# Gated cross-attention and mixture feed-forward: x^T from DRAM, normalized in place, instead of transposes of normalized x

## The chip, the core and the metric

The kernel runs on one core of one Trainium2 chip. A core has a matrix engine (TensorE: PE for its matmuls, PEld for its weight loads), a vector engine (VectorE, DVE), a scalar engine (ScalarE, ACT), a general engine (GpSimd, POOL) and SyncE (SP), which here issues almost all DMAs. Each engine runs its own list of instructions in order and waits for the others through semaphores. The DMAs are carried out by 16 DMA engines. The metric is the device time of one execution in microseconds (us); less is better.

## What is computed

For each of 8 batches, with x of 256 tokens by 512 features and a context of the same shape:

```
x = x + tanh(g0) * attention(layernorm(x), context)
x = x + tanh(g1) * ffn(layernorm(x))

attention(h, c): q = concat(c, h) @ Wq            (32 heads of 16)
                 k, v = h @ Wk, h @ Wv ; ck, cv = c @ Wsk, c @ Wsv   (8 heads of 16)
                 causal window of 64 tokens over both sets of keys, linear bias, softmax
                 output @ Wo
ffn(h):          8 gated (SiLU) basis pieces mixed by a top-4 router, plus a shared gated part
layernorm(x) = (x - mean) / sqrt(var + 1e-5), over the 512 features, without weights
```

Everything is float32. Only the first layernorm, the one ahead of the attention's projections, is touched by the change.

## The kernel before

The host part of the kernel lays some inputs out anew, without arithmetic: the context is handed over already transposed (features by tokens). All matmuls that project x contract over features, so they need normalized x with features on the 128 partitions; this is the tile xnT, 4 blocks of 128 features by 256 tokens, 4 KB in each partition.

**Order of the work.** The kernel writes its instruction order out by hand. Generators (Python functions that yield a cost) emit the instructions of one stage each, and `run` always advances the generator whose time is least. Time is counted in batches: 1.0 is one batch of feed-forward. `start(gen, length, at, total)` stretches a generator so that `total` yielded units take `length` of a batch. Three kinds of generator overlap: `feed_forward(b)` fills the batch's time from b to b + 1; `attention(b + 1)` starts at b - 0.2 and takes 0.86; `project(b + 2)` starts at b + 0.01 (batch 2's at -0.06) and takes 0.62 for 60 units. So in the steady state TensorE alternates between feed-forward blocks of batch b, attention of batch b + 1 and projections of batch b + 2.

**The projections (`project`).** For b of 2 and more: wait until batch b - 3 is stored, load x (L112, 512 KB) and the transposed context ctT (L118, 512 KB) on SP, yield 16 units; then `norm` (L179 to L184): two bn_stats and bn_aggr on DVE, an addition of epsilon on DVE, and a power of -0.5 on POOL; 3 units later `normed` (L190) writes normalized x, two 128x512 tensor_scalar on DVE; 3 units later, for each half of 128 tokens, `transposed` issues four TensorE transposes into one PSUM bank (L204, tile tr_x) and a copy on ACT brings them to xnT (L205). Then come the keys (L532, context first, then xnT), four groups of queries (L584), and the values (L604). All of them share one PSUM bank, `ps_one`, which `hold` and `give` hand from user to user; the tail of the attention (L888 and on) uses it too. Batch 0 is projected by `project_first` and batch 1 by `project` with rows normalized earlier; these keep the transposes.

**Buffers that matter here.** xnT comes from a pool with two buffers (tag "xo") in which it alternates with oT, the attention's output; x has three buffers, ctT one.

**The feed-forward.** Ten pieces a batch, each a set of blocks on TensorE (L1023, L1032) with weight halves that SP loads from DRAM (`load_gu`, L349 and L351). Each weight buffer exists twice: `after` issues the load for piece i + 2 as soon as piece i's last block with that buffer has been emitted. DVE, ACT and POOL follow with sums (L1068, L1079, L1091 on DVE; L1069, L1070 on POOL), tanh (L985 on ACT), gates (L990 on DVE), products (L1108 on DVE) and an accumulation (L1113 on POOL). In batch 0, sums of weights are also made (L975 on DVE and POOL) and kept in DRAM (L979 on SP) for the later batches.

**The attention.** Scores on TensorE (L650) into four PSUM banks; DVE adds the bias and takes the maximum (L663); ACT takes exponentials (L682); DVE's reciprocal (L691) and POOL's multiplication (L694) normalize; DVE transposes 32x32 blocks (L707); TensorE multiplies with the values (L729), which SP has spread into a block-diagonal tile in sixteen DMAs a batch (L496).

Of the kernel before, what the change touches and what calls it, by code (L numbers as in the profile page):

```python
# [9 lines left out]
F32 = mybir.dt.float32  # L10
# [5 lines left out]
P = 128  # L16
# [21 lines left out]
def gated_block(  # L38
    ctx: ExitStack,
    tc: tile.TileContext,  # L40
    x: bass.AP,
    context_t: bass.AP,
    g_xattn: bass.AP,
    g_ffn: bass.AP,
# [65 lines left out]
    def load(b, eng=nc.sync):  # L110
        xt = three.tile([P, NT, HID], F32, tag="x", name=f"x_{b}")
        eng.dma_start(xt, x[b].rearrange("(t p) d -> p t d", p=P))  # L112
        return xt
# [219 lines left out]
    }  # L333

    summed = set()

    def load_gu(i, g):

# [162 lines left out]
    def put_values(pv):  # L501
# [2 lines left out]
            pv.rearrange("p t s (k d) -> p (t s) k d", d=D),  # L504
        )

    def project(b, xns=None):
        def own():
            yield from hold(0.0 if b == 1 else GAP)

        def bank(shape, name):
            return ps_one.tile(shape, F32, tag="one", name=name)

        free = give
        if b > 1:
            while b > 2 and b - 3 not in stored:
                yield 0.5
            loaded[b] = load(b), load_context(b)
            yield 16.0
        xt, ctT = loaded[b]  # L520
        if xns is None:
            normed = norm(xt, range(NT), f"a{b}")
            yield 3.0
            xns = normed()
            yield 3.0
        xnT = two.tile([P, NC, T], F32, tag="xo", name=f"xnT_{b}")
        kT = two.tile([P, 2, 2, T], F32, tag="kT", name=f"kT_{b}")

        def keys(pk, s):
            w_sb, src = ((wsk_sb, ctT), (wk_sb, xnT))[s]  # L530
            for c in range(NC):
                nc.tensor.matmul(  # L532
                    pk[:, s, :], lhsT=w_sb[:, c, :], rhs=src[:, c, :],
                    start=(c == 0), stop=(c == NC - 1),
                )

        if b == 1:

            yield BEFORE
            yield from own()  # L540
            pk = bank([P, 2, T], f"pk_{b}")
            keys(pk, 0)
            for t in range(NT):
                yield MORE
                evict = transposed(
                    xnT, xns[t], t, f"x{b}",
                    lambda shape, name: other_bank(2, name).rearrange("p (c n) -> p c n", n=P),
                )
                yield AFTER
                evict()  # L550
            yield BEFORE
            keys(pk, 1)
            yield AFTER
        else:
            for t in range(NT):
                yield from own()
                evict = transposed(xnT, xns[t], t, f"x{b}", bank)
                yield AFTER - 0.8
                evict()
                free()  # L560
                yield BEFORE + 0.8
            yield from own()
            pk = bank([P, 2, T], f"pk_{b}")
            for s in range(2):
                keys(pk, s)
                yield AFTER

        for par in range(2):
            for s in range(2):
                nc.scalar.activation(  # L570
                    kT[:, par, s, :], pk[:, s, :], AF.Copy, scale=kmask[:, par : par + 1],
                )
        free()
        yield BEFORE
        if b == 1:
            yield BEFORE


        qT = two.tile([P, NB, G, Q], F32, tag="qT", name=f"qT_{b}")
        for g in range(G):  # L580
            yield from own()
            pq = bank([P, T], f"pq_{b}_{g}")
            for c in range(2 * NC):
                nc.tensor.matmul(  # L584
                    pq, lhsT=wq_sb[:, c, g * P : (g + 1) * P],
                    rhs=(ctT if c < NC else xnT)[:, c % NC, :],
                    start=(c == 0), stop=(c == 2 * NC - 1),
                )
                if c % NC == NC - 1:
                    yield MORE if c < NC else AFTER  # L590
            nc.scalar.activation(
                qT[:, :, g, :], pq.rearrange("p (b q) -> p b q", q=Q), AF.Copy, scale=-0.25
            )
            free()
            yield BEFORE
        projected[b] = kT, qT


        yield from own()
        pv = bank([P, NT, 2, HK * D], f"pv_{b}")  # L600
        for t in range(NT):
            for s, (w_sb, src) in enumerate(((wsv_sb, ctT), (wv_sb, xnT))):
                for c in range(NC):
                    nc.tensor.matmul(  # L604
                        pv[:, t, s, :], lhsT=src[:, c, t * P : (t + 1) * P], rhs=w_sb[:, c, :],
                        start=(c == 0), stop=(c == NC - 1),
                    )
            yield AFTER if t else MORE
        put_values(pv)
        free()  # L610
        yield BEFORE
# [668 lines left out]


_INS = [
    "x", "ctx_2048", "g_xattn", "g_ffn",
    "L0_xattn_Wq", "L0_xattn_Wk", "L0_xattn_Wv", "L0_xattn_Wsk", "L0_xattn_Wsv", "L0_xattn_Wo",
    "L0_ffn_w_router", "L0_ffn_w_gate", "L0_ffn_w_up", "L0_ffn_w_down",
    "L0_ffn_amplitudes", "L0_ffn_expert_scale",
# [32 lines left out]
```

## Time and profile before

| | us |
|---|---|
| median of 3 runs | 1020.11 |
| lowest and highest of them | 1019.47 and 1020.87 |
| span of the profiled execution, first to last instruction | 1016.5 |
| what lies around it (median less span) | 3.6 |
| DVE, ACT, POOL busy in that span | 597.9, 441.4, 469.3 |
| TensorE transposes of x (tr_x): 64 matmuls of 128x128, busy in all | 10.1 |
| moved by DMA in that span | 192.15 MB, 189 GB/s |

The profiled execution's own device time is not listed apart from the runs, so its span stands for it. TensorE's granted clock has a mean of 0.988 of full speed. How to read the rows that follow: a group of instructions has its line in the kernel, engine, operation, tiles written and read (out<-in, buffer numbers left out), shapes and count; a row of the timeline has its start and length in us, and in square brackets how long the engine idled just before and what ended that. A row of stretches has its bounds, its length, the busy time of PE, PEld, DVE, ACT and POOL, the granted clock, the DMA engines' busy share and GB/s. The chain of work that ended last is followed back from the last instruction, at each step to what released it.

### The profile page before, as it was taken

How to read it: one execution, taken by the hardware profiler on the slowest of the kernel's cores; microseconds unless marked ns; L12 is line 12 of the kernel's file. 1: busy time of each engine (PE TensorE's matmuls, PEld its weight loads, DVE VectorE, ACT ScalarE, POOL GpSimd, SP SyncE). 2: the span in 40 equal slices, each digit the busy share in tenths (PEclk: the TensorE clock that was granted, in tenths of full speed). 3: DMA queues.
4: the chain of work that ended last, by engine and by line, in shares of the span. 5: the costliest groups of instructions: out<-in, count | busy, mean ns of one | idle time of the engine just before them, and what ended most of it. 6: DMA issues, size and time to landing. Idle time of an engine off the chain costs nothing.

```text
span 1016.5 us, 27831 instructions
## 1 busy us (share of the span) xinstructions
PE 989.0 (97%) x10470; PEld 801.1 (79%) x10470; DVE 597.9 (59%) x2241; ACT 441.4 (43%) x1657; POOL 469.3 (46%) x892
## 2 busy tenths in 40 slices
PE   8899799999999999999999999999999999999998
PEld 8768587867888787886878868787787967787885
DVE  2765666657563775536755377545766466765453
ACT  3653354336542464425643255433654245542231
POOL 4773485635543265423634236432455234661341
PEclk9899799999999999999999999999999999999999
DMA  6943854578444794547844586455864468665891
GB/s 208 239 148 105 222 162 145 178 220 276 155 140 146 201 310 123 166 143 214 270 146 147 167 228 229 137 156 175 268 201 136 146 189 251 205 191 174 275 303 64
DMA packets 117302, 192.15 MB, mean 189 GB/s; under 512 B 12848, under 2 KB 34864, under 8 KB 117168
## 3 DMA queue, kind: packets, MB, share of 16 engines
q1 hardware_dynamic: 112672, 184.87, 58.3%
q10 hardware_dynamic: 4112, 4.46, 1.3%
q8 instruction: 83, 1.36, 0.5%
q0 software_dynamic: 384, 1.05, 0.5%
q14 instruction: 51, 0.42, 0.1%
HBM read 158.87 MB, written 14.68 MB: 171 GB/s over the span
## 4 chain that ended last, share of the span: by engine, by line
PE 88%; DVE 6%; DMA 2%; ACT 2%; POOL 1%; issue 1%; SPq 0%; ACTq 0%; DVEq 0%; POOLq 0%
PE m L1023 37%; PE pq L584 9%; PE m L1032 9%; PE sc L729 6%; PE po L888 5%; PE sc L650 5%; PE pd L1166 4%; PE pv L604 3%; PE pk L532 2%; PE pd L1169 2%; PE pq L402 1%; PE pl L918 1%; DMA ctT<-in_ctx 1%; DVE pr L663 1%; PE tr_f L204 1%; PE tr_x L204 1%
## 5 line engine op out<-in xcount | busy, mean ns | idle before, releaser
L694 POOL TENSOR_SCALAR pr<-pr,rd 128x192 f32<-128x192 f32 (+2 forms) x512 | 209.6, 428 | 228.9 <-DVE rd L691 202.5
L682 ACT ACTIVATE pr<-pr,nm 128x192 f32<-128x192 f32 (+2 forms) x512 | 218.9, 430 | 96.5 <-DVE nm L663 54.0
L1023 PE MATMUL m<-w,sT 128*128 128x256 f32 x1024 | 253.0, 381 | 7.0 <-DMA w<-in_L_ffn_w_up 7.0
L1023 PEld LDWEIGHTS m<-w,sT 128*128 128x128 f32 x1024 | 194.5, 191 | 34.2 <-DMA w<-in_L_ffn_w_up 7.4
L663 DVE CUSTOM_DVE_ANT_1 pr<-sc,nbias 128x192 f32<-128x192 f32 (+2 forms) x512 | 153.9, 322 | 90.3 <-PE sc L650 83.3
L1023 PE MATMUL m<-w,hT 128*128 128x256 f32 x768 | 203.9, 388 | 1.1 <-DVE u L1068 1.0
L1023 PEld LDWEIGHTS m<-w,hT 128*128 128x128 f32 x768 | 139.5, 190 | 25.8 <-issue 6.6
L1113 POOL TENSOR_TENSOR mixed<-mixed,th 128x256 f32<-128x256 f32 x112 | 82.2, 734 | 149.2 <-DVE th L1108 149.2
L707 DVE STREAM_TRANSPOSE pt<-pr 128x768 f32<-128x768 f32 (+2 forms) x128 | 111.5, 871 | 4.0 <-POOL pr L694 3.3
L682 ACT ACTIVATION_READ_ACCUMULATOR pr<-pr,nm 128x1 f32 x512 | 98.0, 191 | 0.0
L985 ACT ACTIVATE th<-m 128x256 f32<-128x256 f32 x80 | 30.8, 386 | 150.9 <-DVE up L1079 150.9
L1069 POOL TENSOR_TENSOR m<-m,u 128x256 f32<-128x256 f32 x80 | 60.6, 757 | 63.9 <-DVE u L1068 54.9
L1091 DVE TENSOR_TENSOR gate<-u,m 128x256 f32<-128x256 f32 x80 | 33.3, 416 | 81.2 <-PE m L1023 71.5
L729 PEld LDWEIGHTS sc<-pt,vbd 64*32 64x32 f32 x5120 | 62.5, 109 | 20.5 <-issue 11.2
L650 PE MATMUL sc<-kT,qT 32*128 32x192 f32 (+2 forms) x1024 | 67.2, 342 | 6.5 <-DVE nm L663 6.1
L729 PE MATMUL sc<-pt,vbd 64*32 64x96 f32 (+2 forms) x5120 | 70.2, 235 | 3.0 <-DVE pt L707 2.1
L1079 DVE TENSOR_TENSOR up<-u,m 128x256 f32<-128x256 f32 x80 | 33.2, 414 | 66.5 <-PE m L1023 40.0
L650 PEld LDWEIGHTS sc<-kT,qT 32*128 32x128 f32 x1024 | 46.7, 187 | 29.1 <-DVE nm L663 9.7
L985 ACT ACTIVATE th<-gate 128x256 f32<-128x256 f32 x80 | 33.3, 417 | 81.7 <-DVE gate L1091 81.6
L1032 PE MATMUL m<-sT,w 128*128 128x128 f32 x512 | 65.1, 275 | 0.0
L1032 PEld LDWEIGHTS m<-sT,w 128*128 128x128 f32 x512 | 61.6, 192 | 0.4
L1070 POOL TENSOR_TENSOR m<-m,m 128x256 f32<-128x256 f32 x80 | 58.5, 731 | 6.3
(131 smaller groups left out, 1373.6 us busy)
## 6 DMA issues: line engine op xcount, KB each, us to landing
w<-s SPq DMA_DIRECT2D x284, 256.0 KB, 3.3
w<-in_L_ffn_w_gate SPq DMA_DIRECT2D x130, 256.0 KB, 3.0
w<-in_L_ffn_w_up SPq DMA_DIRECT2D x73, 256.0 KB, 4.0
vbd<-vpad SPq DMA_DIRECT2D x120, 128.0 KB, 3.0
s<-w SPq DMA_DIRECT2D x40, 256.0 KB, 3.3
w<-in_L_ffn_shared_w_gate SPq DMA_DIRECT2D x32, 256.0 KB, 2.7
w<-in_L_ffn_shared_w_up SPq DMA_DIRECT2D x18, 256.0 KB, 3.5
sd<-in_L_ffn_shared_w_down SPq DMA_DIRECT2D x16, 256.0 KB, 3.6
```

What stands on the lines that cost most here:

```text
L584: nc.tensor.matmul(pq, lhsT=wq_sb[:, c, g * P : (g + 1) * P], rhs=(ctT if c < NC else xnT)[:, c % NC, :], start=(c == 0), stop=(c == 2 * N ...
L650: nc.tensor.matmul(seen(scs[p][:, j * COLS : (j + 1) * COLS], qb), lhsT=qT[rows, qb].rearrange("p g q -> p (g q)"), rhs=kT[rows, par, :, f ...
L663: nc.vector.tensor_tensor_reduce(out=part, in0=seen(scs[p][:, j * COLS : (j + 1) * COLS], qb0 + j), in1=bass.AP(tensor=bias.tensor, offset ...
L682: nc.scalar.activation(part, part, AF.Exp, bias=nmax, scale=-1.0, accum_out=den)
L694: nc.gpsimd.tensor_scalar(part, part, rden[:, p : p + 1], 1.0, op0=ALU.mult, op1=ALU.mult)
L707: nc.vector.transpose(pt[:, u % 4].rearrange("p c (s k) -> p (c s) k", s=2)[:, :, lo:], pr.rearrange("p c (s k) -> p (c s) k", s=2)[:, :, ...
L729: nc.tensor.matmul(scs[gp][32 * c : 32 * (c + 1), 2 * COLS + lo * Q : 2 * COLS + hi * Q], lhsT=vbd[rows, kb % (P // Q), kb // (P // Q) * 2 ...
L985: nc.scalar.activation(th, gate, AF.Tanh, scale=0.5)
L1023: nc.tensor.matmul(dst, lhsT=sides_of[m][c], rhs=w[:, c, :], start=(first and c == 0), stop=(c == NC // 2 - 1), skip_group_check=True,)
L1032: nc.tensor.matmul(dst[:, cols], lhsT=w[:, c, cols], rhs=sides_of[m][c], start=(first and ic == c == 0), stop=(c == NC // 2 - 1), skip_gro ...
L1069: nc.gpsimd.tensor_add(m7, m7, u)
L1113: nc.gpsimd.tensor_add(mixed[t], mixed[t], th)
```

## The change

For batches 2 to 7, x is handed over a second time, transposed by the host (`x_t`), and SP loads it straight into xnT, right behind x and ctT. Row statistics are taken as before from x (tokens on partitions). Mean and reciprocal deviation, 4 values in each partition, are stored to DRAM in an order in which they form one row of 512 values for each batch, and that row is loaded back into all 128 partitions (tile wide, 256 KB). DVE then subtracts the means from xnT in place and POOL multiplies by the deviations, each in two halves of 128x512. The transposes, their copies and the two normalizing instructions are gone for these batches. Seven units lie between the store and the first subtraction, 2.1 behind each half. To make room for wide, the area in SBUF for descriptors of POOL's DMAs is cut to 8192 bytes a partition. Batches 0 and 1 are as before.

```diff
+    rows = {b: sums.tile([NT, 2, P], F32, tag=f"rows{b}", name=f"rows{b}") for b in range(2, B)}
...
+    def norm_transposed(b, xt, xnT):
+
+        stats = small.tile([P, NT, 6], F32, tag="stats", name=f"st_a{b}")
+        mr = small.tile([P, NT, 2], F32, tag="mv", name=f"mv_a{b}")
+        for t in range(NT):
+            nc.vector.bn_stats(stats[:, t, :], xt[:, t, :])
+            nc.vector.bn_aggr(mr[:, t, :], stats[:, t, :])
+        veps = small.tile([P, NT], F32, tag="veps", name=f"ve_a{b}")
+        nc.vector.tensor_scalar(veps, mr[:, :, 1], LN_EPS, None, op0=ALU.add)
+        nc.gpsimd.tensor_tensor(mr[:, :, 1], veps, neghalf, ALU.pow)
+        nc.sync.dma_start(rows[b].rearrange("t s p -> p (t s)"), mr.rearrange("p t s -> p (t s)"))
+        wide = one.tile([P, NT, 2, P], F32, tag="wide", name=f"wide_{b}")
+        nc.sync.dma_start(
+            wide.rearrange("p t s n -> p (t s n)"),
+            rows[b].rearrange("t s p -> (t s p)").partition_broadcast(P),
+        )
+        yield 7.0
+        for half in range(2):
+            part = xnT[:, half * NC // 2 : (half + 1) * NC // 2, :].rearrange(
+                "p c (t n) -> p c t n", t=NT
+            )
+            for which, eng, op in ((0, nc.vector, ALU.subtract), (1, nc.gpsimd, ALU.mult)):
+                row = wide[:, :, which, :]
+                eng.tensor_tensor(
+                    part, part,
+                    bass.AP(
+                        tensor=row.tensor, offset=row.offset,
+                        ap=[list(row.ap[0]), [0, NC // 2], [2 * P, NT], [1, P]],
+                    ),
+                    op,
+                )
+            yield 2.1
...
             loaded[b] = load(b), load_context(b)
+            xnT = two.tile([P, NC, T], F32, tag="xo", name=f"xnT_{b}")
+            nc.sync.dma_start(xnT, x_t[b].rearrange("(c p) t -> p c t", p=P))
             yield 16.0
-        xt, ctT = loaded[b]
-        if xns is None:
-            normed = norm(xt, range(NT), f"a{b}")
-            yield 3.0
-            xns = normed()
-            yield 3.0
-        xnT = two.tile([P, NC, T], F32, tag="xo", name=f"xnT_{b}")
+            xt, ctT = loaded[b]
+            yield from norm_transposed(b, xt, xnT)
+        else:
+            xt, ctT = loaded[b]
+            xnT = two.tile([P, NC, T], F32, tag="xo", name=f"xnT_{b}")
...
         else:
-            for t in range(NT):
-                yield from own()
-                evict = transposed(xnT, xns[t], t, f"x{b}", bank)
-                yield AFTER - 0.8
-                evict()
-                free()
-                yield BEFORE + 0.8
             yield from own()
             pk = bank([P, 2, T], f"pk_{b}")
...
-    nc = bacc.Bacc("TRN2", target_bir_lowering=False, num_devices=1)
+    nc = bacc.Bacc(
+        "TRN2", target_bir_lowering=False, num_devices=1, dynamic_dma_scratch_size=8192
+    )
```

More of the change, by code (lines that the diff above doesn't have):

```diff
@@ L41, in gated_block @@
     x: bass.AP,
+    x_t: bass.AP,
     context_t: bass.AP,
@@ L1282 @@
 _INS = [
-    "x", "ctx_2048", "g_xattn", "g_ffn",
+    "x", "x_t", "ctx_2048", "g_xattn", "g_ffn",
     "L0_xattn_Wq", "L0_xattn_Wk", "L0_xattn_Wv", "L0_xattn_Wsk", "L0_xattn_Wsv", "L0_xattn_Wo",
@@ L1294 @@
     from concourse.bass_utils import run_bass_kernel_spmd
-    nc = bacc.Bacc("TRN2", target_bir_lowering=False, num_devices=1)
+    nc = bacc.Bacc(
+        "TRN2", target_bir_lowering=False, num_devices=1, dynamic_dma_scratch_size=8192
+    )
     arrays, args = {}, []
     for name in _INS:
-        a = np.asarray(inputs[name])
+        a = np.asarray(inputs["x" if name == "x_t" else name])
         if name == "L0_xattn_Wq":
             a = a.reshape(-1, HK, G, D).transpose(0, 2, 1, 3).reshape(a.shape)
-        if name == "ctx_2048":
+        if name in ("ctx_2048", "x_t"):
             a = a.transpose(0, 2, 1)
```

## The prediction

> **What bounds the kernel now.** I read the table of busy times first, then the chain of work that ended last, then a steady stretch of one batch, then TensorE in order of time around the removed transposes. Busy time and chain, from the page:
>
> ```profile
> PE 989.0 (97%) x10470; PEld 801.1 (79%) x10470; DVE 597.9 (59%) x2241; ACT 441.4 (43%) x1657; POOL 469.3 (46%) x892
> ...
> PE 88%; DVE 6%; DMA 2%; ACT 2%; POOL 1%; issue 1%; SPq 0%; ACTq 0%; DVEq 0%; POOLq 0%
> ```
>
> A stretch of 122 us is about one batch. One such row (start:end, length, busy time of PE, PEld, DVE, ACT and POOL with instruction counts, granted clock, DMA share, GB/s):
>
> ```profile
> 474.00:596.00 122.00, 121.52 (x1300) 98.36 (x1299) 72.50 (x277) 55.18 (x208) 52.61 (x103) 1.00 0.61 187
> ```
>
> TensorE is busy for 121.5 of 122 us at full granted clock; the next engine is at 73. In batches 3 to 7, therefore, a matmul that goes is worth its whole time, and other work costs nothing until TensorE waits for it. Before about 130 us this does not hold, as shown below.
>
> **What goes: 48 transposes.** Batch 4's TensorE in order of time (start, duration, line, tiles):
>
> ```profile
> 376.84 1.03 PE L1023 MATMUL m<-w,sT 128*128 128x256 f32 x4
> 377.70 0.60 PE L204 MATMUL tr_x<-ident,xn_a 128*128 128x128 f32 x4
> 378.14 1.03 PE L1023 MATMUL m<-w,hT 128*128 128x256 f32 x4
> 379.18 0.66 PE L204 MATMUL tr_x<-ident,xn_a 128*128 128x128 f32 x4
> 379.77 1.03 PE L650 MATMUL sc<-kT,qT 32*128 32x192 f32 x16
> 380.73 0.89 PE L729 MATMUL sc<-pt,vbd 64*32 64x96 f32 x64
> ```
>
> Matmuls overlap, so I count from start to start. The transposes take 377.70 to 378.14 and 379.18 to 379.77, 0.44 + 0.59. The four L1023 matmuls between them take 1.04 against 0.86 for the same four before them (the second transposes wait for the copy of the first), and the sixteen L650 after them 0.96 against 0.86 elsewhere. That is 0.44 + 0.59 + 0.18 + 0.10 = 1.31 us. Batches 3, 6 and 7 read the same, batch 5 gives 0.44 + 0.56 + 0.06 = 1.06, and batch 2 has 0.44 twice, 0.88. Sum: 4 x 1.31 + 1.06 + 0.88 = **7.2 us**. Also gone are 12 copies on ACT of 586 ns (L205) and 12 normalizations on DVE of 538 ns (L190): ACT is at 43%, so its part is counted at nothing.
>
> **What comes in batches 3 to 7.** Two subtractions on DVE: the nearest row is L975's 128x512 TENSOR_TENSOR, median 685 ns, so 1.37 us against 1.08 that go. Two multiplications on POOL: the same row there is 1275 ns, 2.55 us more. One 512 KB load on SP, a small store, a 256 KB broadcast load. Batch 5 shows what hides them (DVE, POOL, PE):
>
> ```profile
> 492.21 0.69 DVE L179 BATCH_NORM_STATS2 st_a<-x 128x6 f32<-128x512 f32 x1
> ...
> 500.82 0.38 DVE L990 SCALAR_TENSOR_TENSOR th<-th,m 128x256 f32<-128x256 f32 x1
> ...
> 508.96 0.42 DVE L1079 TENSOR_TENSOR up<-u,m 128x256 f32<-128x256 f32 x1 [2.63 <-PE m L1023]
> ```
>
> ```profile
> 494.20 0.88 POOL L184 TENSOR_TENSOR rs_a<-ve_a,neghalf 128x2 f32<-128x2 f32 x1 [2.18 <-DVE ve_a L182]
> ```
>
> ```profile
> 508.76 1.89 PE L532 MATMUL pk<-xnT,wk 128*128 128x256 f32 x8
> ```
>
> The first subtraction is emitted 7.0 steps after the statistics; a step is 0.62/60 of a batch, so 7.0 x 0.62/60 x 122 = 8.8 us, at 492.2 + 8.8 = 501.0 on DVE. The spread statistics must be there by then, and POOL's power ends at 495.1: the store and the load behind it have **5.9 us** before DVE waits. TensorE waits later. From first subtraction to finished x^T is 0.69 (subtract), 1.28 (multiply), 0.73 (an L1113 add in between on POOL), 1.28 = 4.0 us, and TensorE reads xnT at 508.76 - 1.06 = 507.7, so the pair may take 507.7 - 4.0 - 495.1 = **8.6 us** before TensorE loses anything. Behind a waiting DVE stand the softmax steps (L663), the transposes of probabilities (L707) and the gate steps; DVE has the 2.63 us of idle time above to catch up, and POOL 1.9 us before 509.85.
>
> How long the pair takes no row shows. SP's 256 KB loads in this stretch land 2.6 to 4.5 us after issue, which bounds the broadcast. The store has 512 runs of 4 bytes, 32 for each of 16 DMA engines. In the trace's packet records 4-byte packets (nearly all semaphore writes) take 9 ns and 1 KB packets 66 ns, so 0.3 to 2.1 us on top of a landing of 2.4 (the shortest weight load) to 4.5. Pair: 5.3 to 11.1 us. I take 6.5, nearer the small end, since the store moves only 2 KB: DVE waits 0.6 us, TensorE nothing. For the extra 2.55 us on POOL, which is busy from 501.1 to 508.0 without a break, I count 0.1 us a batch, between 0 and 0.5: **0.5 us**. A gain below nothing has no source here, as TensorE idles only 0.3 us a batch.
>
> A rule of the Trainium skill speaks against this store: DMA: Bandwidth & Descriptors, section Rules for kernel authors, says that a non-contiguous last dimension becomes one descriptor per element and should be rearranged. Its section Specifications adds that below 512 B the engine reads, modifies and writes. No run here shows such a store. By the rule, with each of an engine's 32 runs priced as a whole 1 KB packet, the pair would take about 2.8 + 2.1 + 3.3 = 8.2 us, DVE would wait 2.3 us and the sum would stand 0.4 us from growing; with the 9 ns row it stays as it is.
>
> SP stands still at the store until the power is done and at the broadcast until the store has landed, some 2 + 3.4 = 5 us. Queued behind are weight loads (L349, L351). Each refills a buffer that TensorE needs two pieces later (a piece is 8.4 to 9.6 us: L1079 at 490.99, 499.34, 508.96), about 18 us against landings of 2.4 to 7.4: nothing, with some 10 us in hand; past that each us is TensorE's. The x^T load's buffer was last read in the value matmuls of the batch before (done 188.2; load of batch 3 at 236), and ctT's load has that wait already. In these batches its 512 KB are covered by the same 18 us. The halved descriptor area for POOL's DMAs touches eight issues in batch 0; at worst POOL waits there for one landing, 5.0 us. I take nothing.
>
> **Where it costs: batch 2's load.** It falls into batch 0's first feed-forward pieces, where the DMA engines are full (in order: PE, SP's queue, the chain, and two rows of stretches, whose last column but one is the DMA share):
>
> ```profile
> 109.86 1.03 PE L1023 MATMUL m<-w,hT 128*128 128x256 f32 x4
> 117.86 2.07 PE L1023 MATMUL m<-w,sT 128*128 128x256 f32 x4 [6.96 <-DMA w<-in_L_ffn_w_up]
> ```
>
> ```profile
> 107.63 5.86 SPq L496 DMA_DIRECT2D vbd<-vpad  x4
> 113.54 0.59 SPq L349 DMA_DIRECT2D w<-in_L_ffn_w_up  x1
> ```
>
> ```profile
> 103.28 8.88 DMA ctT<-in_ctx
> ```
>
> ```profile
> 108.00:110.00 2.00, 2.00 (x11) 1.77 (x10) 1.91 (x9) 1.97 (x10) 1.73 (x5) 1.00 1.12 273
> 112.00:114.00 2.00, 0.00 (x0) 0.00 (x0) 0.00 (x0) 0.00 (x0) 0.00 (x0) 1.00 0.88 206
> ```
>
> TensorE stands for 6.96 us for a weight load that was issued late, since SP had eight DMAs out and waited for ctT to land. The x^T load goes directly behind ctT and ahead of that weight load. Stretches of 102 to 118 us move 183 to 309 GB/s, so 524 KB take 1.7 to 2.9 us; nothing at all if it found room, but the share is near 1. I take 2.5: **2.5 us lost**. DVE's normalization (1.37 us on the chain at 123.80) no longer stands ahead of the values that TensorE waits 0.55 us for at 126.77: **0.5 us won**.
>
> **Sum.** -7.2 + 0.5 + 2.5 - 0.5 = -4.7 us on a span of 1016.5. The median of the runs, 1020.1, lies 3.6 above the span and I carry the difference over: 1015.4, said as **1015.5 us**.
>
> **Rivals.**
> - The x^T load of batch 2 finds room: -7.2, with the 0.5s cancelling: 1012.9. Against it: the DMA share of 0.88 to 1.13 from 104 us on.
> - Half the gain comes back as waits: POOL's 6.9 us of unbroken work grows by 2.55 and DVE's wait delays score banks. At 0.6 us a batch more, 1015.5 + 6 x 0.6 = 1019.1, no change. For it: TensorE's L650 already waits for DVE 0.32 us at one place in a batch.
> - The pair of transfers is late (the slower side). Place: DVE's first subtraction, with TensorE's L532 on xnT behind it. From 8.6 us each us costs 6 us over six batches; 4.6 us of gain are used up at 8.6 + 0.77 = 9.4 us. At 10 us the time is 1015.5 + 6 x 1.4 = 1023.9. For it: the bound of 11.1; against: two ordinary landings make 5.2 to 9.0.
> - The change does not do what it says: the diff leaves the transposes of batches 0 and 1 alone and removes the rest, so 16 of 64 remain; I give this no more than 0.01.
>
> **Chances.** Forecast 0.50, load hidden 0.12, half given back 0.21, late pair 0.16, nothing done 0.01. A measurement of this kernel can tell about 0.2%, 2.0 us. The forecast's own spread (1.7 to 2.9 us for the load, up to 0.5 a batch for POOL) leaves 0.46 of its 0.50 faster; with the hidden load, faster 0.58. Same: 0.04 + 0.21 + 0.01 = 0.26. Slower 0.16. The range runs from 1012.3 (load hidden and 0.55 won) to 1022.5, where the late pair takes 9.8 us; about 0.15 lies outside.
>
> **What would show it.** Right: tr_x has 16 matmuls left; TensorE's wait near 118 us grows from 7.0 to about 9.5; from 240 us on a batch is 1.0 to 1.3 us shorter than its 121.9; DVE waits under 1 us for the broadcast load. Wrong: the pair takes over 8.6 us and L532 on xnT waits; L1023 waits for weight loads after 240 us (SP held too long); or the wait near 118 us stays at 7.0.

## The result and the profile after

The changed kernel takes **1091.8 us** (median of 4 runs, 1086.7 to 1095.3) against 1019.8 for the kernel before, measured beside it. The ratio is 1.070, 95% interval 1.067 to 1.072. The prediction was 1015.5 us with a range up to 1022.5: the sign was wrong, and the size far outside the range. The profiled execution of the changed kernel took 1086.7 us, 1084.9 of them span, against the span of 1016.5 before: 68.4 us to explain.

In the profile after, the lines from the queries on stand 28 lines later than before (scores L678, bias and maximum L691, mixing L757, feed-forward L1051); the new steps are L514 to L518 (statistics and power), L519 (store), L521 (broadcast load) and L532 (subtraction and multiplication); the keys are L567. The busy times and the chain, from its page:

```profile
PE 999.9 (92%) x10422; PEld 807.5 (74%) x10422; DVE 603.7 (56%) x2241; ACT 436.7 (40%) x1645; POOL 483.0 (45%) x904
...
PE 78%; DMA 10%; DVE 8%; ACT 2%; POOL 1%; issue 1%; SPq 1%; ACTq 0%; DVEq 0%; POOLq 0%
```

TensorE lost its 48 transposes and is yet busy for 10.9 us more; and it idles for 1084.9 - 999.9 = 85.0 us instead of 27.5. DMA, at 2% of the chain before, has 10%. So there are two things to find: what TensorE waits for, and why its matmuls got slower. The list of waits (who, for whom, us in total, times, longest), first the engines, then SyncE's queue:

```profile
PE sc L678 <- DVE nm L691: 59.1, 15, 9.8
...
DVE xnT L532 <- DMA wide<-rows: 45.2, 5, 10.3
...
DVE xnT L532 <- DMA w<-s: 9.2, 1, 9.2
```

```profile
SPq L521 <- DMA rows<-mv_a: 47.4, 6, 8.3
SPq L519 <- POOL mv_a L518: 12.6, 6, 5.7
```

The last DVE row is batch 3's wait: it ends as the broadcast load lands, too (5.8 us behind its issue), though the view names a weight load for it. So DVE waits 54.4 us in all six batches. TensorE does not wait for xnT, as the forecast had it, but for DVE's maxima of the scores. The three engines in batch 5, in order of time, SP, DVE, then PE (start, length, and in brackets the idle time before):

```profile
529.55 0.37 SPq L519 DMA_DIRECT2D rows<-mv_a  x1
538.28 0.32 SPq L521 DMA_DIRECT2D wide<-rows  x1
538.64 0.43 SPq L351 DMA_DIRECT2D w<-in_L_ffn_w_up  x1
```

```profile
543.95 0.69 DVE L532 TENSOR_TENSOR xnT<-xnT,wide 128x512 f32<-128x512 f32 x1 [9.21 <-DMA wide<-rows]
544.56 0.35 DVE L691 CUSTOM_DVE_ANT_1 pr<-sc,nbias 128x192 f32<-128x192 f32 x1
```

```profile
535.03 0.59 PE L678 MATMUL sc<-kT,qT 32*128 32x192 f32 x4
544.97 1.92 PE L678 MATMUL sc<-kT,qT 32*128 32x192 f32 x12 [9.35 <-DVE nm L691]
546.82 1.29 PE L757 MATMUL sc<-pt,vbd 64*32 64x96 f32 x64
548.04 3.40 PE L1051 MATMUL m<-w,sT 128*128 128x256 f32 x8
551.28 1.89 PE L567 MATMUL pk<-ctT,wsk 128*128 128x256 f32 x8
```

POOL's power ends at 529.52. The store takes 8.7 us to land, only then does SP issue the broadcast load, and that takes 5.65: 14.4 us, with DVE standing at L532 for 9.2 of them. Behind L532 in DVE's list stand the softmax steps (L691). They empty the four score banks, and the next scores need an empty bank: DVE stops at 534.74, TensorE at 535.62, and it starts again at 544.97, as the first maximum is through. It stands for 9.35 us, as long as DVE. The keys that read xnT come at 554.73 and wait for nothing.

Then the clock. The eight L1051 matmuls at 548.04 take 3.40 us; eight of them took 1.89 at 528.89. Two stretches (start:end, length, busy time of PE, PEld, DVE, ACT, POOL, granted clock, DMA share, GB/s):

```profile
545.00:549.00 4.00, 4.00 (x78) 3.38 (x79) 4.00 (x12) 1.84 (x7) 3.64 (x4) 0.50 1.01 377
...
560.00:660.00 100.00, 98.69 (x1049) 78.98 (x1048) 54.26 (x209) 40.75 (x154) 38.04 (x77) 1.00 0.61 185
```

The clock granted behind the standstill is half (0.50), and it is whole again some 6 us later.

The sum over the span, read from one batch's first key matmul to the next one's: up to batch 2's keys 144.83 us instead of 134.11 (10.7 more), from batch 2's to batch 3's 140.5 instead of 127.5 (13.0 more), then four batches of 133.04 instead of 121.83 (44.8 more), and behind batch 7's keys 0.2 less: 68.4 in all. In the middle four a batch without any wait would take 121.83 - 1.31 = 120.5; TensorE's waits in them are 8.20, 9.35, 9.76 and 8.15 us (mean 8.9), which leaves 133.0 - 120.5 - 8.9 = 3.6 us a batch behind the waits. Most of it is the clock: TensorE works 4.0 to 6.6 us a batch at half clock there, which by itself costs half of that, 2.0 to 3.3 us (mean 2.8). The other 0.8 is not assigned.

The first two stretches have the same cause for the most part. The 10.7 us up to batch 2's keys are TensorE's two waits for maxima there, 6.84 and 0.91, and the growth of its wait for weights near 118 us from 6.96 to 9.80: 10.6 together. The 13.0 us behind them hold batch 3's wait of 9.35 with its clock, as in the four batches that follow (11.2 each), and 1.8 more.

### The profile page after: what moved, and what is told of

Its sections match the earlier page's. It is cut to its first block, busy times and chain, and to the rows that moved or that the text cites. A ratio compares the mean times of both kernels' runs of the same rounds, so it can differ in the third digit from the quotient of the medians.

```text
span 1084.9 us, 27794 instructions
## 1 busy us (share of the span) xinstructions
PE 999.9 (92%) x10422; PEld 807.5 (74%) x10422; DVE 603.7 (56%) x2241; ACT 436.7 (40%) x1645; POOL 483.0 (45%) x904
## 4 chain that ended last, share of the span: by engine, by line
PE 78%; DMA 10%; DVE 8%; ACT 2%; POOL 1%; issue 1%; SPq 1%; ACTq 0%; DVEq 0%; POOLq 0%
PE m L1051 31%; PE pq L612 9%; PE m L1060 9%; PE sc L757 6%; PE sc L678 5%; PE po L916 5%; DMA rows<-mv_a 5%; PE pd L1194 4%; DMA wide<-rows 3%; PE pv L632 2%; PE pk L567 2%; PE pd L1197 2%; DVE pr L691 1%; DMA vbd<-vpad 1%; PE pq L404 1%
## 5 line engine op out<-in xcount | busy, mean ns | idle before, releaser
L722 POOL TENSOR_SCALAR pr<-pr,rd 128x192 f32<-128x192 f32 (+2 forms) x512 | 207.1, 423 | 228.4 <-DVE rd L719 202.5
L1051 PE MATMUL m<-w,sT 128*128 128x256 f32 x1024 | 259.2, 388 | 9.8 <-DMA w<-in_L_ffn_w_up 9.8
L1051 PEld LDWEIGHTS m<-w,sT 128*128 128x128 f32 x1024 | 198.9, 195 | 38.8 <-DMA w<-in_L_ffn_w_up 10.2
L1051 PE MATMUL m<-w,hT 128*128 128x256 f32 x768 | 204.1, 388 | 2.0 <-DVE u L1096 1.0
L691 DVE CUSTOM_DVE_ANT_1 pr<-sc,nbias 128x192 f32<-128x192 f32 (+2 forms) x512 | 153.8, 322 | 88.8 <-PE sc L678 82.3
L1051 PEld LDWEIGHTS m<-w,hT 128*128 128x128 f32 x768 | 140.0, 191 | 27.3 <-issue 7.7
L678 PE MATMUL sc<-kT,qT 32*128 32x192 f32 (+2 forms) x1024 | 77.0, 358 | 59.5 <-DVE nm L691 59.1
L678 PEld LDWEIGHTS sc<-kT,qT 32*128 32x128 f32 x1024 | 53.0, 196 | 85.2 <-DVE nm L691 64.3
L757 PEld LDWEIGHTS sc<-pt,vbd 64*32 64x32 f32 x5120 | 63.8, 111 | 21.1 <-issue 12.4
L757 PE MATMUL sc<-pt,vbd 64*32 64x96 f32 (+2 forms) x5120 | 71.8, 239 | 2.6 <-DVE pt L735 2.5
L1194 PE MATMUL pd<-sd,shT 128*128 128x512 f32 x128 | 61.3, 601 | 0.0
```

The lines of the kernel that those rows point to most:

```text
L678: nc.tensor.matmul(seen(scs[p][:, j * COLS : (j + 1) * COLS], qb), lhsT=qT[rows, qb].rearrange("p g q -> p (g q)"), rhs=kT[rows, par, :, f ...
L691: nc.vector.tensor_tensor_reduce(out=part, in0=seen(scs[p][:, j * COLS : (j + 1) * COLS], qb0 + j), in1=bass.AP(tensor=bias.tensor, offset ...
L722: nc.gpsimd.tensor_scalar(part, part, rden[:, p : p + 1], 1.0, op0=ALU.mult, op1=ALU.mult)
L757: nc.tensor.matmul(scs[gp][32 * c : 32 * (c + 1), 2 * COLS + lo * Q : 2 * COLS + hi * Q], lhsT=vbd[rows, kb % (P // Q), kb // (P // Q) * 2 ...
L1051: nc.tensor.matmul(dst, lhsT=sides_of[m][c], rhs=w[:, c, :], start=(first and c == 0), stop=(c == NC // 2 - 1), skip_group_check=True,)
L1194: nc.tensor.matmul(po, lhsT=shT[:, ic, t * P : (t + 1) * P], rhs=down[ic], **flags)
```

## The experiments

Two theories stood at the start. **Wait:** DVE's standstill at the subtraction, passed on through the score banks, is the whole loss. **Held queue:** SP standing still at the store and at the load makes weight loads late, and DVE's wait hides that. Beside them was the question why the pair takes 14 us. Batch lengths below are means of the same four batches (before 121.83, after 133.04).

**Subtraction later (e1_time).** Statistics and store 3 units earlier, and 16 units instead of 7 from there to the subtraction, which so comes 6 later:

```diff
-            yield 16.0
+            yield 13.0
...
-        yield 7.0
+        yield 16.0
```

> Statistics 3 units earlier, first subtraction 6 units later, so the store and the broadcast load have about 17 us instead of 5.9. If the late pair is the whole cause, DVE's wait for the broadcast (9 us a batch) and TensorE's waits of 8 to 10 us at the scores go, TensorE's clock stays at 1.00, and the time is 1015 to 1019 us. If the cause is SP held at the store for 8.5 us (weight loads late), or the extra work on DVE and POOL, the time stays above 1050 us.

Measured: 1056.9 us, ratio 1.035 (1.031 to 1.040), batch 129.1. DVE's waits for the broadcast are 7.4 us in all instead of 54.4, and yet half of the loss is there. What TensorE now waits for:

```profile
PE m L1051 <- DMA w<-in_L_ffn_w_up: 27.3, 6, 7.4
...
PE pk L567 <- DVE x L921: 6.5, 5, 1.3
```

The first is the late weights of the theory of the held queue (7.4 at the start, where it was 6.96 before the change, and 1.6 to 5.9 in each of the others); the second, 1.3 us in each batch, came with the keys' later place in TensorE's list (it is gone in e12, where they have their old place). Neither theory alone is enough.

**Fewer and longer runs (e2_runs16).** The four values of a row as one run of 16 bytes, 128 runs instead of 512; DVE and POOL then read wide with a step:

```diff
-        nc.sync.dma_start(rows[b].rearrange("t s p -> p (t s)"), mr.rearrange("p t s -> p (t s)"))
+        nc.sync.dma_start(rows[b].rearrange("p t s -> p (t s)"), mr.rearrange("p t s -> p (t s)"))
```

> Mean and deviation stored as one run of 16 bytes a partition (128 runs instead of 512 of 4 bytes); order of all instructions unchanged. If the store is slow by its number of runs, it lands in about 2.4 + 6.1/4 = 4 us instead of 8.5, the pair in 9.6, TensorE waits some 4 us a batch instead of 9 and the time is 1030 to 1055 us. If it is slow because many small writes fall into the same stretch of DRAM, however long the runs, it stays near 8 us and the time near 1090 us.

Measured: 1051.4 us, 1.030 (1.027 to 1.033), batch 126.50. The store lands after 3.4 us instead of 8.5 (medians), the load after 4.4; DVE waits 17.0 us in all. TensorE's waits at the scores in batches 3 to 7 are 2.0 to 3.7 us, each half a us longer than DVE's (1.5 to 3.2), since the subtraction ahead of the softmax steps is slower, too (1.07 us instead of 0.69). Nearly half of the pair's time was the form of the store.

**No wait for the store (e4_nowait).** The broadcast load takes its row from x instead of the stored statistics, the same work with other numbers, so it need not wait for the store:

```diff
-            rows[b].rearrange("t s p -> (t s p)").partition_broadcast(P),
+            x[0, 0, :].partition_broadcast(P),
```

> The broadcast load takes a row of x instead of the stored statistics, so it doesn't wait for the store (the normalization uses wrong numbers; the work is the same). Late pair: the load lands some 6 us after the power, DVE waits under 1 us, no TensorE wait over 1 us from 240 us on, 1015 to 1020 us. If the broadcast alone is what is late, TensorE still waits several us a batch and the time is over 1035 us.

Measured: 1068.3 us, 1.048 (1.044 to 1.051), batch 129.59. The list of DMA issues (KB, median us from issue to landing):

```profile
wide<-in_x SPq DMA_DIRECT2D x6, 256.0 KB, 9.9
...
rows<-mv_a SPq DMA_DIRECT2D x6, 2.0 KB, 10.4
```

The first branch of the expectation missed; the second has the time, but not the reason. The load is issued 0.4 us behind the store and lands with it, some 10.3 us behind the store's issue, where the pair took 14.1 with the wait between them. So that wait is the smaller part of the price: the store's small writes hold up the load by themselves.

**Which stores are slow (e3_probe, e16_apart).** The kernel before, with stores and loads on ScalarE's queue that nobody waits for; the form of the store changes from batch to batch (here packed, and apart by n values):

```diff
+            nc.scalar.dma_start(dense[b].rearrange("t s p -> p (t s)"), mv.rearrange("p t s -> p (t s)"))
...
+            nc.scalar.dma_start(far[b][:, :, :, 0].rearrange("t s p -> p (t s)"), mv.rearrange("p t s -> p (t s)"))
```

> The kernel before, with stores and broadcast loads that nobody waits for, issued on ACT's queue. Store forms by batch: 2: 512 runs of 4 bytes, dense; 3: 128 runs of 16; 4: 512 of 4, 64 bytes apart; 5: 512 of 4, 512 bytes apart; 6: 128 runs of 4; 7: 256 runs of 8. By number of runs: 8.5, 4, 8.5, 8.5, 4, 5.5 us. By collisions in one stretch of DRAM: about 8 dense, and the spaced ones clearly shorter. Broadcast loads some 50 us after the stores: 5.6 us if 128 reads of the same 2 KB are slow by themselves, 3 us if only freshly written rows are; the plain 256 KB load of batch 5 about 3 us.

> The kernel before with one unread store of the statistics per batch on ScalarE's queue, 512 runs of 4 bytes each time: 64 bytes apart in batches 2, 4 and 7, packed in batches 3 and 5, 16 bytes apart in batch 6. If the number of runs sets the time, all six land alike, 8 to 10 us behind their issue. If packed neighbours do: packed 8 to 11 us, 64 bytes apart 3.5 to 5, 16 bytes apart between them. Time 1018 to 1022 us, since nobody waits for them.

Times 1020.1 and 1020.9 us, one run each: unwaited, they cost nothing that shows. The trace counts a DMA's 16 completions; from issue to the last one, in us (with a "+", not all 16 were recorded, and the last one seen stands there):

```
512 runs of 4 B, packed          10.50   10.4+   10.9+
512 runs of 4 B, 16 B apart       4.72
512 runs of 4 B, 64 B apart       4.25    3.79    4.42    3.54
512 runs of 4 B, 512 B apart      4.91
128 runs of 4 B, packed           8.5+
256 runs of 8 B, packed           6.8+
128 runs of 16 B, packed          4.56
256 KB broadcast load, row stored by the kernel    4.24    3.58    4.27    3.65
256 KB broadcast load, row of x                    3.75
256 KB plain load                                  2.76
```

The number of runs is not what counts: the same 512 runs land in 3.5 to 4.9 us when they are 16 bytes or more apart. Packed side by side they take over 10, and 128 of them still over 8. This corrects what e2 seemed to say. That a row was stored by the kernel itself (60 us or more earlier here) does not slow its load by more than half a us against a row of x.

The same traces show that the packed store holds up more than its own queue. In e16 it was issued on ScalarE's queue; a 256 KB weight load went out on SyncE's queue 0.05 us behind it in batch 3 (first block, packed) and in batch 4 (second block, 64 bytes apart):

```profile
257.11 0.41 ACTq L518 DMA_DIRECT2D dense<-mv_a  x1
...
257.16 0.32 SPq L360 DMA_DIRECT2D w<-s  x1
```

```profile
379.03 0.40 ACTq L518 DMA_DIRECT2D far<-mv_a  x1
...
379.08 0.32 SPq L360 DMA_DIRECT2D w<-s  x1
```

By its completions the first weight load took 9.4 us or more (14 of 16 recorded), the second 4.0; a weight load issued 5 us behind the packed store still took 8.6. So what is busy with the packed writes is shared by both queues. The batches behind e16's two packed stores, from one's first key matmul to the next one's, still took 121.9 and 122.7 us.

**Steps pulled apart (e5_apart), batch 2 left as it was (e6_old2).** 16-byte runs; statistics after 10 units, store 5 behind, load 5 behind, subtraction 6 behind. In e6 batch 2 keeps its transposes too:

```diff
-            yield 16.0
+            yield 10.0
...
+        yield 5.0
         nc.sync.dma_start(rows[b].rearrange("p t s -> p (t s)"), mr.rearrange("p t s -> p (t s)"))
+        yield 5.0
...
-        yield 7.0
+        yield 6.0
```

> The changed kernel with the four values of a row stored as one run of 16 bytes, and with the steps pulled apart: statistics after 10 units of matmul work instead of 16, the store 5 units behind them, the broadcast load 5 behind the store, the first subtraction 6 behind the load. If the loss has three parts (VectorE standing still before the subtraction, SyncE standing still before the two DMAs with the weight loads behind it, the slower start), the first two go: no wait of TensorE over 1 us in batches 3 to 7, and 1012 to 1019 us. If SyncE's standstill costs nothing and the weights come late in the version with the later subtraction for another reason (more bytes, the x^T load), waits for weights of 3 to 6 us per batch stay, and it takes 1025 to 1040 us.

> The same, but batch 2 keeps the transposes of normalized x and loads no x^T. If the x^T load of batch 2 is what makes the weights at 118 us late, TensorE's wait there goes back from some 9 to 7 us, for 0.9 us of transposes: 1 to 2 us faster than the version that differs from it in batch 2 alone, 1011 to 1017 us. If that wait is longer for another reason, it is 1 us slower than that version.

Measured: 1036.4 (1.015; 1.013 to 1.018) and 1030.8 us (1.010; 1.008 to 1.013), batches of 123.56 and 124.87. Neither expectation held: e5's time falls into its second branch, but without the late weights that were to cause it. SP is hardly held any more (0.4 us in all in e5), and no wait for weights is left behind batch 2. But in this place the load lands after 5.5 and 6.3 us (medians), later than DVE gets to the subtraction, which still waits 1.0 to 3.4 us a batch. In e5's batch 2 SP, late with what stands ahead in its queue, issued the store only 7.7 us after the power, and TensorE's keys waited 5.49 us for POOL's multiplication: this is what e6 wins back, not the wait near 118 us, which is 8.4 in e6.

**The load of x^T alone (e7_load), the pair alone (e8_hold).** The kernel before, transposes and all. In e7 x^T is loaded into the buffer that the transposes then overwrite; in e8 the 4-byte store and the broadcast load stand on SP's queue as in the changed kernel, and nobody reads wide:

```diff
+            xnT = two.tile([P, NC, T], F32, tag="xo", name=f"xnT_{b}")
+            nc.sync.dma_start(xnT, x_t[b].rearrange("(c p) t -> p c t", p=P))
             yield 16.0
```

```diff
+        if to is not None:
+            nc.sync.dma_start(to.rearrange("t s p -> p (t s)"), mv.rearrange("p t s -> p (t s)"))
+            wide = one.tile([P, NT, 2, P], F32, tag="wide", name=f"wide_{name}")
+            nc.sync.dma_start(
+                wide.rearrange("p t s n -> p (t s n)"),
+                to.rearrange("t s p -> (t s p)").partition_broadcast(P),
+            )
```

> The kernel before plus the load of x^T alone: 512 KB into the buffer that the transposes then overwrite, so nothing is taken out. If the load costs at the start alone: TensorE's wait near 118 us 7.0 to 9.0-9.8 us, no new wait later, 1022 to 1024 us. If its traffic also makes weights late in each batch: over 1026 us. If the start's longer wait came from something else: 1020 us.

> The kernel before plus the two DMAs of the statistics on SyncE's queue, at the place that the changed kernel gives them, with 512 runs of 4 bytes and the load waiting for the store; nobody reads what is loaded, so VectorE has no new wait and nothing is taken out. If SyncE's standstill alone makes the weights late: waits for w_up or w_gate of 2 to 6 us in batches 2 to 7 and 1030 to 1045 us. If all of the loss is VectorE's wait: 1020 to 1022 us.

Measured: e7 1021.6 us (1.002; 1.0005 to 1.0039), batch 121.90; e8 1038.5 us (1.019; 1.017 to 1.022), batch 123.31. So x^T's 512 KB cost some 1.7 us (0.5 to 4.0 by the interval), at the start alone (the wait near 118 us is 9.28), and nothing later. The pair on SP's queue costs 18.6 us with no wait of DVE for it at all: in e8's profile some 7.5 of them are lost by 207 us, and the rest behind it, with waits for weights of up to 2.6 us a batch. We read this as the price of SP's standstill more than of the slow writes, since e16's packed stores on the other queue delayed weight loads as well, for under 1 us a batch. The wait of SP's queue that does it, at the load behind the store (us in total, times, longest):

```profile
SPq L191 <- DMA rows<-mv_a: 56.5, 6, 10.0
```

**More room (e9_later), another queue (e10_actq, e11_actq_old2).** e9 is e6 with `yield 10.0` instead of `yield 6.0` ahead of the subtraction. e10 and e11 are e5 and e6 with the pair on ScalarE's queue:

```diff
-        nc.sync.dma_start(rows[b].rearrange("p t s -> p (t s)"), mr.rearrange("p t s -> p (t s)"))
-        yield 5.0
+        nc.scalar.dma_start(rows[b].rearrange("p t s -> p (t s)"), mr.rearrange("p t s -> p (t s)"))
+        yield 6.0
...
-        nc.sync.dma_start(
+        nc.scalar.dma_start(
```

> The version with batch 2 by transposes, its first subtraction 10 units behind the broadcast load instead of 6. The load was seen to land 5.7 to 7.1 us behind its issue there, and VectorE waited 1.9 to 3.4 us. If that wait is what is left of the loss in batches 3 to 7, it goes, with TensorE's waits of 1.7 to 3.2 us behind the scores: 1014 to 1020 us, ten us or more faster than that version. If the rest of the loss is the traffic of the added loads or the other order of the steps: 1026 to 1032 us, no change.

> The version with the steps pulled apart in all of batches 2 to 7, its store and its broadcast load issued on ScalarE's queue, in which nothing else is loaded at this time, and 6 units between them. If the load is slow there because it stands behind weight loads in SyncE's queue, it lands some 4 us behind its issue as in the unused loads on this queue, and VectorE and TensorE wait no more in batches 3 to 7; in batch 2, where SyncE was 8 us late with the store, neither. 1014 to 1020 us. If the load is slow because all queues share the DMA engines: VectorE waits 1 to 2 us as before, 1030 to 1036 us.

> The same with batch 2 by transposes and without its x^T load. The load's price at the start was 1.7 us of time and 2.3 us of TensorE's wait near 118 us, the transposes of batch 2 cost 0.9 us: 0.5 to 2 us faster than the version before it, 1012 to 1019 us. This is the version that might beat both kernels.

Measured: 1024.2 (1.004; 1.003 to 1.006), 1027.9 (1.007; 1.005 to 1.009) and 1025.2 us (1.004; 1.003 to 1.006), batches of 122.71, 122.11 and 122.69. All three expectations missed their times. DVE does not wait at the subtraction in batches 3 to 7 of any of them. What the missing transposes free is gone all the same. In e10's batch 5:

```profile
494.83 1.15 PE L759 MATMUL sc<-pt,vbd 64*32 64x96 f32 x64 [0.87 <-DVE nm L693]
530.60 1.56 PE L614 MATMUL pq<-ctT,wq 128*128 128x256 f32 x6 [0.92 <-DVE x L923]
```

The first stands right behind DVE's statistics, which now fall between softmax steps that TensorE needs; the second behind the attention's output projection, whose bank the queries share, because keys and queries come later in TensorE's list. 0.87 + 0.92 = 1.79 against 1.31 freed. One batch from its first key matmul to the next one's, before and in e10:

```profile
383.40:505.30 121.90, 121.42 (x1299) 98.29 (x1298) 72.48 (x278) 55.10 (x206) 52.58 (x104) 1.00 0.60 187
...
393.50:515.50 122.00, 120.21 (x1291) 96.88 (x1290) 75.19 (x278) 54.32 (x205) 58.05 (x106) 1.00 0.63 192
```

TensorE has 1.2 us less to do and idles 1.8 us instead of 0.5. So a batch of e10 is only 0.3 us longer than before, and most of its 8 us are lost earlier: up to batch 3's keys TensorE idles 7.8 us more, with waits of 3.57 and 5.24 us around 118 us (6.96 before) and of 1.97 for POOL's multiplication in batch 2.

The broadcast load landed after 5.4 us on this queue, too, so the weights ahead of it in SP's queue were not what made it slow in e5. It was no slower than its neighbours: weight loads issued within 3 us of batch 5's took 4.2 to 6.4 us on SP's queue. Nor was it slow for having been stored just before: in e8, issued as the store landed, it took 3.3 to 4.5 us in batches 3 to 7. What it shares with the weights is the DMA engines, at a busy share of 0.91 from 504 to 510 us.

**The order of before (e12_order, e13_split, e14_early).** From e11, with 27.2 units between loads and keys, as in the changed kernel, instead of 31.2. TensorE's list is then that of the kernel before without the removed transposes. e13 has the statistics after 8 units with `yield 0.6` between their two tiles, e14 after 7. The edit of e12:

```diff
-                yield 10.0
+                yield 9.2
...
-        yield 5.0
+        yield 4.0
...
-        yield 6.0
+        yield 5.0
...
-        yield 6.0
+        yield 5.0
```

> The version with ScalarE's queue and batch 2 by transposes, with 27.2 units of matmul work from the loads to the keys instead of 31.2 (statistics after 9.2, store after 4, load after 5, subtraction after 5, the halves 2 apart): TensorE's instructions are then in the order of the kernel before, without the transposes of batches 3 to 7. If the other order of the matmuls eats what the transposes free, the waits of 0.9 us at the queries go: 1018 to 1022 us; if traffic or something else eats it, 1024 to 1028 us. VectorE may wait up to 1 us for the load.

> The same order, with the statistics after 8 units and their two tiles 0.6 units apart, so that softmax steps get in between, and the subtraction 6 units behind the load. If the statistics' place costs the 0.87 us at the mixing matmuls, that wait gets smaller or goes: 1014 to 1019 us; otherwise as the version with the statistics after 9.2.

> The same order, with the statistics after 7 units, undivided, and 5.6 and 6.4 units behind the store and the load. 1014 to 1021 us if the order is what counts, 1024 to 1028 us if not; with a wait of VectorE for x in each batch, if x lands later than 7 us.

Measured: 1038.1 (1.017; 1.015 to 1.019), 1027.3 (1.007; 1.004 to 1.009; 1022.4 to 1033.6) and 1037.2 us (1.017; 1.015 to 1.018). All three missed: the wait at the queries is gone, but the earlier statistics now wait for x itself, which lands 3.7 to 6.1 us behind its issue, up to 5.4 us in a batch (e14). DVE in e13, and TensorE in e12, behind a subtraction that waited 1.74 us for the broadcast load:

```profile
487.76 0.69 DVE L514 BATCH_NORM_STATS2 st_a<-x 128x6 f32<-128x512 f32 x1 [2.10 <-DMA x<-in_x]
```

```profile
514.06 1.19 PE L694 MATMUL sc<-kT,qT 32*128 32x192 f32 x12 [1.96 <-DVE nm L707]
```

The chain x, statistics, store, load, normalization did not fit between the load of x and the keys' old place in any of the three; each version pays at another link, and none of them beats the kernel before. Loading x earlier was not tried.

**DVE's wait alone (e15_wait).** The same order; pair on ScalarE's queue, subtraction right behind the load:

```diff
-                yield 10.0
+                yield 16.0
...
-        yield 5.0
+        yield 2.0
...
-        yield 6.0
+        yield 5.0
...
-        yield 6.0
+        yield 0.0
```

> The same order, with VectorE's wait put back by itself: statistics after 16 units as in the changed kernel, store 2 behind, broadcast load 5 behind, both on ScalarE's queue so that SyncE is not held, and the subtraction right behind the load. The load lands 5 to 6 us behind its issue, so VectorE waits some 5 us in each of batches 3 to 7. If that wait is passed on to TensorE through the softmax steps queued behind it: waits of 4.5 to 6 us at the scores, half the clock behind them, 6 to 8 us per batch, 1048 to 1062 us. If TensorE has the 2.6 us of slack that the forecast read from the keys: waits of some 2.5 us, 1030 to 1038 us.

Measured: 1060.9 us (1.040; 1.038 to 1.042), batch 129.51. TensorE waits for no weights behind batch 2. Waits and a stretch behind the wait in batch 5:

```profile
PE sc L694 <- DVE nm L707: 33.8, 13, 6.3
...
DVE xnT L534 <- DMA wide<-rows: 25.2, 5, 5.8
```

```profile
522.50:526.00 3.50, 3.50 (x77) 3.00 (x78) 3.50 (x11) 1.55 (x6) 3.14 (x3) 0.50 0.20 68
```

DVE waits 4.6 to 5.8 us a batch and TensorE 5.1 to 6.3: passed on whole, and half a us more, since the subtraction itself (1.06) stands ahead of the softmax steps. In the four batches of the mean they are 5.13, 5.09, 5.54 and 5.75, mean 5.4, and 129.5 - 120.5 - 5.4 = 3.6 us behind the waits, as in the changed kernel (2.9 of it by the half clock). So a batch costs its wait plus 3.6, for waits of 5 and of 9 us; e2, with 3.2, leaves 126.5 - 120.5 - 3.2 = 2.8 (1.7 by the half clock). One reservation: in this run too SP waited 23.2 us for the load's semaphore, but no matmul waited for what it held back.

## Why the prediction was wrong, point by point

- **"A matmul that goes is worth its whole time": held for TensorE's work, but nowhere seen as a gain.** 1.31 us a batch were counted, and in e10 TensorE's busy time fell by 1.2; every version gave it back in waits.
- **"I take 6.5" for the pair: a term too small by more than a factor of two, and beyond its upper bound of 11.1.** Measured 14.1 (medians 8.5 and 5.6). The store was bounded by 9 ns and 66 ns packets; its packets do show 9 ns each, and batch 5's last is sent 3.0 us behind the issue, but the completion comes 8.7 us behind it. Here the packets in the records bound the sending, not the landing. The load was bounded by weight loads of 2.6 to 4.5; it takes 3.6 to 4.3 on a quiet queue and 5 to 6 in this place, where a plain load of as many bytes took 2.8 on the quiet queue.
- **The 8.6 us "before TensorE loses anything", with L532 on xnT as the place of its wait: the step that failed.** It followed xnT to the keys and asked when TensorE needs what DVE is waiting to make. What counted is what stands behind the waiting instruction: the softmax steps were named there, and 2.63 us of later idle time on DVE taken as enough to catch up. But TensorE needs the next maximum within about 1 us (it stopped at 535.6, 0.9 us after DVE did), so DVE's wait is passed on whole. Its own rival, late pair at "each us costs 6 us" past 8.6, would have given 1015.5 + 6 x 5.5 = 1048 us even with the right 14.1. The wrong path needed the wrong term to do its harm: DVE reached batch 5's subtraction 5.2 us behind the power (529.5 to 534.7), so a pair of 6.5 us would have held it 1.3 us, by the same rows.
- **The clock was left out.** Behind its wait, 8.9 us in the mean, a batch lost 3.6 more, some 2.8 of it in matmuls at half clock.
- **SP's hold "nothing, with some 10 us in hand": wrong.** SP stood 2.1 us a batch at the store and 7.9 at the load (12.6 and 47.4 over six) instead of the 5 counted, and e8 prices the pair on SP's queue at 18.6 us by itself. In the changed kernel TensorE has no wait for weights in batches 3 to 7; that its standstill covers them is our reading, and e1, with most of DVE's wait gone, has these waits.
- **x^T's load in batch 2, 2.5 us: right in mechanism, a little too large.** The wait near 118 us went from 6.96 to 9.80 (9.28 with the load alone), for 1.7 us in the time. That its 512 KB cost nothing in later batches held (121.90 against 121.83).
- **0.5 us won at 126.77, 0.5 us lost on POOL:** neither can be told apart under waits of 9 us. POOL's multiplication took the 1.27 us forecast. The row of POOL that was read as unbroken from 501.1 to 508.0 has a break of 0.20 us at 506.42.
- **The Trainium skill's rule** in DMA: Bandwidth & Descriptors, Rules for kernel authors, against a non-contiguous last dimension spoke against this store, and the trace agrees that this one was bad: 8.5 us against 3.4 for contiguous 16 bytes. But the runs put the price elsewhere than on the one descriptor per element that it names: 512 single elements 64 bytes apart took 3.5 to 4.4.

The loss of 68 us on the span is thus shown in its mechanism (e15, e2 and e4: wait plus clock; e1 and e8: the held queue under it). The 0.8 us a batch and the 1.8 us ahead of batch 3's keys that are not assigned stay open, and why packed 4-byte writes complete so late and hold up the loads of both queues, too.

## What to carry to other kernels

Before an instruction on an in-order engine gets a DMA to wait for, look at what is queued behind it and how soon the bound engine needs that: here the consumer of the waiting result had 8 us, and the next instruction in line had one. A DRAM round trip for a small vector is two landings in a row, here some 8 us with 16-byte runs (e2) and 14 as written; its queue, its waiting issuer and its place in the order each have a price, so it needs its own run before it replaces 1.3 us of matmul. Do not write 4-byte values side by side from many partitions (10.4 to 10.9 us here): leave room between them (3.5 to 4.9) or write the values of a partition as one run (4.6).

## What the runs showed of the hardware

- Small stores to DRAM: 512 runs of 4 bytes packed side by side completed 10.4 to 10.9 us after issue on a quiet queue, the same 512 runs 16, 64 or 512 bytes apart after 3.5 to 4.9. A load issued behind such a store in the same queue landed with it (e4, medians of 9.9 and 10.4 us), and weight loads issued behind it on the other queue took 8.6 to over 10 us, behind a store 64 bytes apart 3.9 to 4.6 (e16).
- The clock of TensorE: behind a wait of 1.96 us at the scores (e12) the next stretch ran at half clock; behind 0.87 and 0.92 us (e10) at the whole clock, and behind a wait of 3.17 us ahead of the mixing matmuls (e6, batch 4) at the whole clock, too. The rows of e12 and e6 for the stretch behind the wait, with the granted clock in the last column but two:

```profile
516.00:519.00 3.00, 3.00 (x17) 2.40 (x9) 3.00 (x9) 0.91 (x3) 3.00 (x3) 0.50 0.11 38
...
389.00:393.00 4.00, 3.81 (x77) 3.32 (x78) 3.81 (x14) 2.46 (x11) 2.89 (x3) 1.00 0.17 37
```

Over all these traces, from 230 us on, no wait of TensorE under 1.6 us was followed by half clock, and every one of 3.6 us or more was; between them some were (1.62 in e12, 1.77 in e5) and some were not (2.30 in e13, 3.17 in e6), and what decides there is not shown. The Trainium skill, TensorE: Matmul & The Clock Gate, Why this matters for your kernels, advises against idle gaps over some 3 us between bursts. Here 1.62 us could be enough and 3.17 could pass, so the measurement asks for more care than the page.
